# First attention in 32 steps per image, with the scores of a unit beside the weighing of the one before it, across images

## The chip, the core and the metric

The kernel runs on one core of one Trainium2 chip. The metric is the device time of one execution in microseconds, as the median of several runs. The profile is of one further execution, with its own time.

## What is computed

Eight images of 32 x 32 positions and 256 channels pass two layers. The first normalises each image in groups of eight channels and adds, to the input, a 3 x 3 convolution (192 channels) and an attention with eight heads of width 8 (64 channels):

```
logits = einsum('bnid,bnjd->bnij', qf, kf)
logits = logits + rel_w + rel_h          # from rel = einsum('bnxyd,md->bnxym', q, rel_k), in x and in y
weights = softmax(logits, axis=-1)
attn = einsum('bnij,bnjd->bnid', weights, vf)
x = x + concat([conv_out, attn @ attn_w + attn_b])
```

The second layer takes the 1024 positions as tokens: layer norm, one attention head of width 128 with a residual, then a mixture of eight experts of which each image uses two, and a last layer norm. The experts are a separate stage behind all images, and the change leaves it alone.

## The kernel before

Everything up to the experts lies in one hand-ordered program: the order of calls in the source is the order on each engine. Image after image goes through `first_layer` (L676) and `second_layer` (L803).

**The first attention.** Query times key and both relative terms are one matmul. Queries, their products with the relative tables and the maxima stand as rows of a feature tile F (128 rows, two key halves, four heads, 512 queries); keys and one-hot rows stand in KM. An image has four units (two halves of the queries, two groups of four heads). A unit (`Unit`, L493) first loads F from DRAM with six DMAs. `score` (L516) makes the logits of 128 queries of one head in PSUM (two matmuls, L522) and VectorE takes their maximum (L529); a unit has 16 scores. `fold` (L533) splits the maxima, turns them and writes them into F with four DMAs (L548). `weigh` (L553) makes the logits once more, transposed and with the maximum taken off (L558), and ScalarE takes the exponential (L565); a unit has eight steps of four weighings. `gather` (L567) multiplies with the values (four column groups at once, L573), and `settle` (L584) divides.

**The steps.** `first_layer` runs over steps. Step s has two scores of unit s // 8 and four weighings of the step that lies ten steps back (`lead = NT + LAG`). Twelve scores of an image's first unit are already taken beside the second attention of the image before, so its steps run from 6 to 42: four with scores alone, 22 with both, ten with weighings alone, one last. Between them `fill.send(us)` puts in other matmuls: the convolution of this and then of the next image (`convolve_tile`, L477, 36 matmuls of fp32 as the profile counts them, one PSUM bank for all), and chains of small work: `token_mean` of the image before, `normalise` of the next (from step 12, L302), `project` (L610), which makes the inputs of the second attention from half an image.

**The features.** After the weighings, `queries` (L381) copies the queries out of the tile kqh into the tile scr (eight DMAs, L388) and to DRAM (four, L395), and GpSimd makes a second order of them (L400). `keys` (L405) loads the next image's keys into KM with four DMAs of eight rows (L407). `features` (L411) multiplies the queries with the relative tables: per group of heads and per direction 32 small matmuls into a two-bank tile `lg`, two ScalarE copies of the high part (L436), two VectorE subtractions for the low part (L437), and stores to DRAM (L440, L444) from a tile of which there are three. These pieces stand between the matmuls of the second attention, where ScalarE and VectorE have its softmax.

**Queues and buffers.** Nearly all DMAs are issued on SP, in program order: a DMA that waits holds those behind it. PSUM has two double banks `lg`, two banks `st` for weighings, one `mi` for convolution and values, one `po`. SBUF has three tiles of F's size, which go round among units, scr and the projected queries and keys of the second attention:

```
        def f_tile(name, dt=FR):
            return work.tile([P, 2, HG, 512], dt, tag="F", name=name, bufs=3)
```

Of the kernel before, what the change touches and what calls it, by code (L numbers as in the profile page):

```python
# [38 lines left out]
def kernel(  # L39
# [67 lines left out]
    with ExitStack() as ph:  # L107
# [30 lines left out]
        def f_tile(name, dt=FR):  # L138
            return work.tile([P, 2, HG, 512], dt, tag="F", name=name, bufs=3)
# [241 lines left out]
        def queries(b):  # L381
            kqb_ = ready.pop(b)
            scr = f_tile("scr").rearrange("p w h s -> p (w h s)")
            qs = scr[:, 0 : 2 * S].rearrange("p (g s) -> p g s", g=NG)
            qx = scr[:, 2 * S : 4 * S].rearrange("p (g s) -> p g s", g=NG)
            for g in range(NG):
                for i in range(4):
                    nc.sync.dma_start(  # L388
                        out=qs.bitcast(FP)[32 * i : 32 * i + 32, g],
                        in_=kqb_[DK + 32 * g : DK + 32 * g + 32, i // 2, :],  # L390
                    )
            fd = fds[b % 2]
            for g in range(NG):
                for c in range(2):
                    nc.sync.dma_start(  # L395
                        out=fd[g].rearrange("(l c p) s -> c p l s", c=2, p=32)[c, :, 0:2],
                        in_=kqb_[DK + 32 * g : DK + 32 * g + 32],
                    )
            for g in range(NG):
                nc.gpsimd.tensor_copy(  # L400
                    qx[:, g].rearrange("p (x y) -> p y x", y=HH), qs[:, g].rearrange("p (y x) -> p y x", x=WW)
                )
            return qs, qx

        def keys(b):  # L405
            for i in range(4):
                nc.sync.dma_start(  # L407
                    out=KMb[8 * i : 8 * i + 8], in_=kds[b % 2][i % 2].rearrange("(d h) s -> d h s", h=NH)
                )

        def features(b, qs, qx):  # L411


            for g in range(NG):
                for which in range(2):
                    pr = lg_tile("prel").rearrange("p a s -> p (a s)")
                    tab, src = ((bhs, qs), (bws, qx))[which]
                    for i in range(32):
                        nc.tensor.matmul(  # L419
                            pr[:, i * 32 : (i + 1) * 32],  # L420
                            lhsT=tab[:, (WW - 1 - i) * HG : (2 * WW - 1 - i) * HG],
                            rhs=src[:, g, i * 32 : (i + 1) * 32],
                            start=True,
                            stop=True,
                        )
                        if i == 15:
                            yield None
                    t = pt_tile("rel", FR).rearrange("p (l s) -> p l s", l=2)
                    for half in range(2):
                        c = slice(half * 512, (half + 1) * 512)  # L430
                        if which == 0:
                            ps, hi, lo = pr[:, c], t[:, 0, c], t[:, 1, c]
                        else:
                            ps = pr.rearrange("p (x y) -> p y x", y=HH)[:, half * 16 : half * 16 + 16, :]
                            hi, lo = (t[:, l, c].rearrange("p (y x) -> p y x", x=WW) for l in range(2))
                        nc.scalar.copy(hi, ps)  # L436
                        nc.vector.tensor_tensor(lo, ps, hi, ALU.subtract)  # L437
                    tb = t.bitcast(FP)
                    if which == 0:
                        nc.sync.dma_start(out=fys[b % 2][g].rearrange("l p s -> p l s"), in_=tb)  # L440
                    else:
                        dst = fds[b % 2][g][R_M * HG : (R_M + 64) * HG].rearrange("(l p) s -> p l s", p=P)
                        for p in (slice(HG, 64), slice(64, P)):
                            nc.sync.dma_start(out=dst[p], in_=tb[p])  # L444
                    yield None
# [47 lines left out]
        class Unit:  # L493


            def __init__(self, b, n):
                self.half, self.g = divmod(n, NG)
                g, cols = self.g, slice(self.half * 512, self.half * 512 + 512)
                self.F = f_tile("F")
# [101 lines left out]
        class Second:  # L601


            def __init__(self, b):
                big = f_tile("nqk", FP).rearrange("p w h s -> p (w h s)")
                self.nT = big[:, 0 : 2 * S].rearrange("p (k s) -> p k s", k=KC)
                self.qk = big[:, 2 * S : 4 * S].rearrange("p (i s) -> p i s", i=2)
                self.v = work.tile([P, NT, U], FP, tag="v1", name="v1")
# [65 lines left out]
        LAG = 2  # L674

        def first_layer(b, units):  # L676
            at = work.tile([P, NT, DK], FP, tag="at", name="at")
            if b > 0:
                fill.chains.append(token_mean(b - 1))
            sec = None  # L680
            more = b + 1 < B
            lead = NT + LAG
            for s in range(units[0].scored // 2, NU * NT + lead + 1):
                u, j = divmod(s, NT)
                w, k = divmod(s - lead, NT)
                g, l = divmod(s - lead - 1, NT)
                score, weigh = u < NU, 0 <= w < NU
                if s % NT == 0 and 0 < u <= NU:
                    units[u - 1].fold()
                    if u < NU - 1:  # L690
                        units.append(Unit(b, u + 1))
                if s == 12 and more:
                    T[b + 1] = load_image(b + 1)
                    fill.chains.append(normalise(b + 1))
                if s == 3 * NT + 4:
                    sec = Second(b)
                    fill.chains.append(project(b, at, sec, 0, (2, 4, 2)))
                if s == 4 * NT + 3 and more:
                    while b + 1 not in ready:
                        fill.send(0.4)  # L700
                    qs = queries(b + 1)
                us = 0.45
                if done[b] < NT:
                    us = max(us, (NT - done[b]) * 3.2 / max(22 - s, 1))
                if score:
                    units[u].score()
                if weigh:
                    units[w].weigh(k, 0)
                if not score:
                    fill.send(0.2)  # L710
                if score:
                    units[u].score()
                if weigh:
                    units[w].weigh(k, 1)
                if score:
                    fill.send(us)
                if 0 <= g < NU:
                    units[g].gather(l)
                if weigh:
                    units[w].weigh(k, 2)  # L720
                if g > 0 and l == 0:
                    units[g - 1].settle(at)
                fill.send(us if score else 0.4)
                if weigh:
                    units[w].weigh(k, 3)
# [3 lines left out]
            rel = None  # L729
            if more:  # L730
                keys(b + 1)
                rel = features(b + 1, *qs)
            fill.send(1.2)
            if more:
                next(rel)
            units[NU - 1].settle(at)
            fill.send(1.2)
            for c in project(b, at, sec, 1, (1, 6, 1)):
                if c is None:
                    fill.send(1.0)  # L740
            if more:
                next(rel)
            return sec, rel

        class Attention:
# [37 lines left out]
            def drain(self, ahead):  # L783
                while self.scored:
                    self.turn()
                    ahead(2)
                while self.turned:
                    self.turned.pop(0).finish()

# [13 lines left out]
        def second_layer(b, sec, rel):  # L803
            more = b + 1 < B
            st2 = work.tile([P, NT, 6], FP, tag="lst2", name="lst2")
            units = []
            if more:
                fill.dense.insert(min(1, len(fill.dense)), values(b + 1))
            pieces = [2]

            def beside():
                if more and pieces[0] < 8:
                    next(rel)
                    pieces[0] += 1
                    if pieces[0] in (4, 8):
                        units.append(Unit(b + 1, pieces[0] // 4 - 1))
                    fill.send(0.6)
                else:
                    ahead(2)

            def ahead(n):
                for _ in range(n if units else 0):
                    units[0].score()
                fill.send(0.6)

            att.beside = beside
            for ib in range(S // IB):

                def finish(pt, rc, ib=ib):
# [7 lines left out]
                    if ib >= 2:  # L837
                        ahead(2)
                    else:
                        fill.send(0.8)  # L840
# [14 lines left out]
            ahead(2)  # L855
            att.drain(ahead)
            sums[b] = st2
            return units
# [36 lines left out]
        with tc.manual_schedule():  # L895
# [4 lines left out]
            rel = features(0, *queries(0))  # L900
            keys(0)
            fill.dense.insert(min(1, len(fill.dense)), values(0))
            units = []
            for g in range(NG):
                for i in range(4):
                    fill.send(1.5)
                    next(rel)
                units.append(Unit(0, g))
            fill.send(5.0)
            for b in range(B):  # L910
                sec, rel = first_layer(b, units)
                units = second_layer(b, sec, rel)
# [275 lines left out]
```

## Time and profile before

| | us |
|---|---|
| median of 3 runs (2893.95 to 2902.46) | 2897.83 |
| the profiled execution | 2906.21 |
| its span, first to last instruction | 2904.4 |
| first weighing of image 0, of images 2 and 4 | 143.7, 729.5, 1299.5 |
| end of the second attention of image 7 | 2356.3 |
| mean clock granted to TensorE, of full speed | 0.96 |

One core has five engines that run on their own and wait for each other by semaphores: PE (TensorE, with PEld for its weights), DVE (VectorE), ACT (ScalarE), POOL (GpSimd) and SP, which here issues DMAs. The page gives each engine's busy time and the chain of work that ended last. A stretch table gives the busy time of each engine between two moments, with the number of instructions in brackets, the granted clock, the mean busy share of the 16 DMA engines and the GB/s moved. A row of the timeline has start, length, engine, line, operation, what is written from what, how many in a row, and in brackets the idle time of the engine ahead of it with what ended it.

### The profile page before, as it was taken

The numbers are of one execution on the slowest core, as the hardware profiler recorded it, in microseconds if no ns is written. First come the engines' busy times: TensorE is split into PE (matmuls) and PEld (weight loads), VectorE is DVE, ScalarE is ACT, GpSimd is POOL, SyncE is SP. The second block draws the span as 40 slices with busy tenths as digits, with TensorE's granted clock in tenths as the row PEclk, the third lists the DMA queues.
The fourth block names the chain that finished last, engine by engine and source line by source line (L and its number), as shares of the span: only waits on it lengthen the run. The fifth ranks groups of instructions, "written<-read, shape, count | busy, mean of one in ns | idle before, by whom it ended". The sixth has DMA issues, their size and how long they took to land.

```text
span 2904.4 us, 30948 instructions
## 1 busy us (share of the span) xinstructions
PE 2560.5 (88%) x12395; PEld 1685.4 (58%) x12395; DVE 1296.2 (45%) x2327; ACT 965.3 (33%) x1679; POOL 301.0 (10%) x196
## 2 busy tenths in 40 slices
PE   4899879997998799979987998799889769999998
PEld 3865665565656555655475556555654346666665
DVE  4454256426643564366335634662457252333232
ACT  0045214531452145214521552154225422223222
POOL 3011001100110011001100110011000021111110
PEclk7899889999999999999999999999999989999999
DMA  3621233133313321342144114312421031112110
GB/s 99 140 56 38 65 80 74 29 70 94 71 31 80 90 56 31 87 97 42 30 90 99 38 36 95 88 38 41 108 55 30 1 106 58 58 58 73 58 51 22
DMA packets 89761, 186.12 MB, mean 64 GB/s; under 512 B 8161, under 2 KB 36714, under 8 KB 87314
## 3 DMA queue, kind: packets, MB, share of 16 engines
q1 hardware_dynamic: 86962, 182.04, 26.6%
q8 instruction: 98, 1.61, 0.2%
q10 hardware_dynamic: 2656, 2.10, 0.2%
q14 instruction: 45, 0.37, 0.0%
HBM read 112.15 MB, written 62.52 MB: 60 GB/s over the span
## 4 chain that ended last, share of the span: by engine, by line
PE 76%; DVE 15%; ACT 5%; DMA 2%; issue 2%; SPq 1%; POOL 0%; ACTq 0%; DVEq 0%
PE pc L481 11%; PE po L573 9%; PE st L558 9%; PE py L1115 8%; PE phd L1097 8%; DVE mx L529 6%; PE lg L522 6%; PE prel L419 4%; PE po L832 4%; PE lg L754 3%; PE pq L653 2%; ACT PT L565 2%; PE tp L772 2%; PE pmean L874 1%; DMA T<-in_x_dram 1%
## 5 line engine op out<-in xcount | busy, mean ns | idle before, releaser
L565 ACT ACTIVATE PT<-st 128x512 f32<-128x512 f32 x1024 | 598.5, 598 | 492.5 <-PE st L558 452.9
L529 DVE TENSOR_REDUCE mx<-lg 128x1 f32<-128x1024 f32 x512 | 603.7, 1217 | 296.0 <-PE lg L522 295.9
L481 PE MATMUL pc<-convw,gpad 128*128 128x192 f32 x2304 | 506.0, 341 | 55.1 <-DVE T L489 33.6
L558 PE MATMUL st<-F,KM 128*128 128x512 f32 x1024 | 479.7, 474 | 19.6 <-ACT PT L565 11.6
L481 PEld LDWEIGHTS pc<-convw,gpad 128*128 128x128 f32 x2304 | 404.3, 196 | 109.5 <-DVE T L489 42.7
L522 PE MATMUL lg<-KM,F 128*128 128x512 f32 x1024 | 345.5, 424 | 73.9 <-ACT pr L760 32.9
L558 PEld LDWEIGHTS st<-F,KM 128*128 128x128 f32 x1024 | 192.2, 190 | 297.3 <-ACT PT L565 177.4
L573 PE MATMUL po<-PT,vk 128*32 128x512 f32 x2048 | 284.0, 617 | 0.0
L522 PEld LDWEIGHTS lg<-KM,F 128*128 128x128 f32 x1024 | 184.4, 190 | 143.0 <-DVE mx L529 50.3
L1115 PE MATMUL py<-w,hT 128*128 128x256 f32 x1024 | 237.3, 385 | 0.0
L1097 PE MATMUL phd<-n2T,w 128*128 128x512 f32 x512 | 222.9, 593 | 0.0
L1115 PEld LDWEIGHTS py<-w,hT 128*128 128x128 f32 x1024 | 189.9, 190 | 45.6 <-issue 22.4
L1122 DVE TENSOR_TENSOR r<-py,n 128x256 f32<-128x256 f32 x64 | 27.2, 425 | 308.4 <-PE py L1115 308.4
L1097 PEld LDWEIGHTS phd<-n2T,w 128*128 128x128 f32 x512 | 97.0, 191 | 115.5 <-issue 108.4
L352 POOL TENSOR_TENSOR T<-T,l0b 128x2048 f32<-128x2048 f32 x8 | 36.5, 4558 | 1145.2 <-PE tpx L311 1145.2
L591 DVE RECIPROCAL rc<-pa 128x16 f32<-128x16 f32 x32 | 8.3, 258 | 307.1 <-PE pa L588 307.1
L760 ACT ACTIVATE pr<-lg,nm 128x1024 f32<-128x1024 f32 x64 | 71.4, 1115 | 201.8 <-DVE nm L758 201.8
L754 PE MATMUL lg<-nqk 128*128 128x512 f32 x256 | 129.8, 633 | 0.0
L437 DVE TENSOR_TENSOR rel<-prel,rel 128x512 fp32r<-128x512 f32 x64 | 44.3, 692 | 190.6 <-ACT rel L436 190.6
L641 POOL TENSOR_TENSOR T<-T,n 128x256 f32<-128x256 f32 x64 | 48.3, 774 | 755.1 <-DVE n L638 755.1
L832 PE MATMUL po<-pt,v 128*128 128x256 f32 x512 | 121.1, 391 | 0.4 <-DVE pt L775 0.4
L1104 ACT ACTIVATE hT<-phd,b1c 128x512 f32<-128x512 f32 x128 | 86.3, 686 | 97.6 <-PE phd L1097 97.4
(223 smaller groups left out, 2441.4 us busy)
## 6 DMA issues: line engine op xcount, KB each, us to landing
F<-fd SPq DMA_DIRECT2D x64, 768.0 KB
fy<-rel SPq DMA_DIRECT2D x16, 1024.0 KB
F<-fy SPq DMA_DIRECT2D x128, 128.0 KB
w<-in_L_ffn_W_dram SPq DMA_DIRECT2D x32, 512.0 KB
T<-in_x_dram SPq DMA_DIRECT2D x8, 1024.0 KB
scr<-kqh SPq DMA_DIRECT2D x64, 128.0 KB
fd<-kqh SPq DMA_DIRECT2D x32, 256.0 KB
KM<-kd SPq DMA_DIRECT2D x32, 256.0 KB
```

Of the source, the lines that this page charges most:

```text
L419: nc.tensor.matmul(pr[:, i * 32 : (i + 1) * 32], lhsT=tab[:, (WW - 1 - i) * HG : (2 * WW - 1 - i) * HG], rhs=src[:, g, i * 32 : (i + 1) * 32],
L481: nc.tensor.matmul(pc[:, 0:CO], lhsT=gflat[:, dx, kc, t * P + dy * WW : (t + 1) * P + dy * WW], rhs=convw[:, (dy * 3 + dx) * KC + kc, :], ...
L522: nc.tensor.matmul(lg[:, a, :], lhsT=self.F[:, a, hl, i * P : (i + 1) * P], rhs=KM[:, self.g * HG + hl, a * 512 : (a + 1) * 512], start=Tr ...
L529: nc.vector.tensor_reduce(self.mx[:, i, hl : hl + 1], lg.rearrange("p a s -> p (a s)"), AX.X, ALU.max, negate=True)
L558: nc.tensor.matmul(st, lhsT=KM[:, self.g * HG + hl, j * P : (j + 1) * P], rhs=self.F[:, j // 4, hl, :], start=True, stop=True,)
L565: nc.scalar.activation(self.pts[j][:, hl, :], st, AF.Exp)
L573: nc.tensor.matmul(self.po[32 * hl : 32 * hl + 32, :], lhsT=vk[:, j, (self.g * HG + hl) * (DH + 1) : (self.g * HG + hl) * (DH + 1) + 32], ...
L754: nc.tensor.matmul(lg[:, h, :], lhsT=q, rhs=k[:, h * 512 : (h + 1) * 512], start=True, stop=True)
L832: nc.tensor.matmul(po[:, 0:IB], lhsT=sec.v[:, jc, :], rhs=pt[:, jc, :], start=jc == 0, stop=jc == NT - 1)
L1097: nc.tensor.matmul(phd, lhsT=ws[k][0][:, kc, f * P : (f + 1) * P], rhs=n2T[:, kc, q * 512 : (q + 1) * 512], start=kc == 0, stop=kc == KC - 1,)
L1104: nc.scalar.activation(hT[:, k * NF + f, :], phd, AF.Gelu, bias=b1c[:, f, k * B + b : k * B + b + 1])
L1115: nc.tensor.matmul(py, lhsT=hT[:, k * NF + f, j * P : (j + 1) * P], rhs=ws[k][1][:, f, :], start=False, stop=k == TOPK - 1 and f == NF - 1,)
```

## The change

The first attention has now 34 steps. In steps 0 to 31 each has four weighings. The two scores of a step run four scores and one unit ahead: unit 1 in steps 0 to 5, unit 2 in 6 to 13, unit 3 in 14 to 21, none in 22 to 25, and unit 0 of the next image in 26 to 33; four scores of its unit 1 follow in the last part of the second attention. To make this possible, the features of the next image move out of the second attention into the fillings of steps 16 to 23, as eight pieces of 16 matmuls. A piece writes one half of what was a double bank, into the single bank `mi`, and the tile `rel` of high and low parts is now one and takes the place of kqh. `keys` is split by groups of heads: group 0 at step 24, group 1 behind the steps. The next image is loaded and normalised from step 0 on, and the convolution must be finished by step 10. The three tiles of F's size have fixed places, `slot % 3`, in place of going round: the next image's queries take the place of unit 1 at step 16, its unit 0 the place of unit 2 at step 24. Before the first image, all features are made, then twenty scores.

```diff
-        def f_tile(name, dt=FR):
-            return work.tile([P, 2, HG, 512], dt, tag="F", name=name, bufs=3)
+        def f_tile(name, slot, dt=FR):
+            return work.tile([P, 2, HG, 512], dt, tag=f"F{slot % 3}", name=name)
...
+        def place(b, n):
+            return n - b
+
+        def keys(b, g):
+            hs = slice(g * HG, (g + 1) * HG)
             for i in range(4):
                 nc.sync.dma_start(
-                    out=KMb[8 * i : 8 * i + 8], in_=kds[b % 2][i % 2].rearrange("(d h) s -> d h s", h=NH)
+                    out=KMb[8 * i : 8 * i + 8, hs],
+                    in_=kds[b % 2][i % 2].rearrange("(d h) s -> d h s", h=NH)[:, hs],
                 )
...
+        def features(b, qs, qx, n):
+            g, which, half = n // 4, n // 2 % 2, n % 2
+            if half == 0:
+                rels[b] = work.tile([P, 2, S], FR, tag="kqh", name="rel")
+            t = rels[b]
+            pr = mi_tile("prel")
...
+            for i in range(16 * half, 16 * half + 16):
+                nc.tensor.matmul(
...
+                if i % 16 < 15:
+                    yield 0.118
...
+            nc.scalar.copy(hi, ps)
+            nc.vector.tensor_tensor(lo, ps, hi, ALU.subtract)
+            if half == 1:
...
+            done["rel", b] = n + 1
+            yield 0.118
...
-        LAG = 2
+        AHEAD = 4
...
+            for s in range(NU * NT + 2):
+                n = AHEAD + 2 * s
+                u, first = n // 16 + 1, n % 16 == 0
+                if s >= 22:
+                    u, first = NU, s == 22
+                score = u < NU or more and 26 <= s < 34
+                weigh, g = s < NU * NT, s - 1
+                gather = 0 <= g < NU * NT
+                if s == 0:
+                    units.append(Unit(b, 2))
+                    if b > 0:
+                        fill.chains.append(token_mean(b - 1))
+                    if more:
+                        fill.chains.append(fetch(b + 1))
+                        fill.chains.append(normalise(b + 1))
+                if first and s > 0:
                     units[u - 1].fold()
+                if s == 8:
+                    units.append(Unit(b, 3))
+                if s == 16 and more:
                     while b + 1 not in ready:
                         fill.send(0.4)
                     qs = queries(b + 1)
+                    i = min(1, len(fill.dense))
+                    for n in range(8):
+                        fill.dense.insert(i + n, features(b + 1, *qs, n))
+                if s == 24:
+                    while more and done.get(("rel", b + 1), 0) < 8:
+                        fill.send(0.5)
+                    if more:
+                        keys(b + 1, 0)
+                        units.append(Unit(b + 1, 0))
+                    sec = Second(b)
+                    fill.chains.append(project(b, at, sec, 0, (2, 6, 2)))
                 us = 0.45
                 if done[b] < NT:
-                    us = max(us, (NT - done[b]) * 3.2 / max(22 - s, 1))
+                    us = max(us, (NT - done[b]) * 3.3 / max(10 - s, 1))
+                if more and 16 <= s < 24:
+                    us = 1.05
...
             if more:
-                keys(b + 1)
-                rel = features(b + 1, *qs)
...
+                keys(b + 1, 1)
+                units.append(Unit(b + 1, 1))
...
             def beside():
...
+                fill.send(1.2)
+
+            def ahead():
+                if more and units[1].scored < AHEAD:
+                    units[1].score()
+                    units[1].score()
+                fill.send(1.0)
```

## The prediction

> **What bounds the kernel now.** I read the page first: busy shares, then the chain that ended last.
>
> ```profile
> PE 2560.5 (88%) x12395; PEld 1685.4 (58%) x12395; DVE 1296.2 (45%) x2327; ACT 965.3 (33%) x1679; POOL 301.0 (10%) x196
> PE 76%; DVE 15%; ACT 5%; DMA 2%; issue 2%; SPq 1%; POOL 0%; ACTq 0%; DVEq 0%
> ```
>
> TensorE is the bound; no other engine is half busy. So a stage is worth the time in which TensorE does not advance. Ends of matmuls are modelled, so I price by distances between starts in the timeline:
>
> ```profile
> 1052.73 0.39 PE L558 MATMUL st<-F,KM 128*128 128x512 f32 x1
> 1052.96 0.81 PE L481 MATMUL pc<-convw,gpad 128*128 128x192 f32 x4
> 1053.70 1.07 PE L573 MATMUL po<-PT,vk 128*32 128x512 f32 x8
> 1054.70 0.50 PE L558 MATMUL st<-F,KM 128*128 128x512 f32 x1
> ```
>
> A scoring or weighing matmul takes 0.23 us, a convolution matmul 0.16, a gather group (eight rows) 1.2 with its hand-over. Other starts give: feature matmul 0.11, transposes 0.11, lg of the second attention and projections 0.43, po and pa there 0.215. Times the counts of one image (128 st, 128 lg, 288 pc, 32 groups, 128 prel, 56 of 0.43, 96 of 0.215, and 240 small ones of 0.11) this is 230 us. Image after image (weigh starts at 729.5 and 1299.5, two apart) takes 285. So 55 us an image are lost. The stretch table says where (image 3):
>
> ```profile
> core 0: us, PE busy (x) PEld busy (x) DVE busy (x) ACT busy (x) POOL busy (x), PEclk, DMA share, GB/s
> 988.80:1016.80 28.00, 21.02 (x86) 12.75 (x85) 16.60 (x34) 0.94 (x4) 0.00 (x0) 0.88 0.39 104
> 1016.80:1130.10 113.30, 104.34 (x555) 65.68 (x554) 72.88 (x100) 54.89 (x97) 16.32 (x12) 0.97 0.19 36
> 1130.10:1168.80 38.70, 36.53 (x190) 17.80 (x190) 2.28 (x5) 24.89 (x44) 4.02 (x2) 1.00 0.25 56
> 1168.80:1196.60 27.80, 24.81 (x154) 20.05 (x149) 7.61 (x25) 2.75 (x6) 5.37 (x5) 1.00 0.30 38
> 1196.60:1271.00 74.40, 64.45 (x347) 49.68 (x347) 38.47 (x59) 19.53 (x35) 0.00 (x0) 0.98 0.47 113
> ```
>
> Scores alone (ACT 0.94 us busy), scores and weighing, weighing alone (DVE 2.28), the tail, second attention. Length less priced work: 12.5, 15.5, 5.5, 5.3, 14.3 us lost.
>
> **What it gives, per image.** Scores alone: gone but for two steps and four late scores, 12.5 to 1: 11.5. Steps: of 15.5 + 5.5, steps 0 to 17 lose 7.5 (normalisation, convolution tiles), which stays; the projection in steps 18 to 22 loses 9.3 beside a fold, later in steps 24 to 29 perhaps 3.7; weighing alone 0.4 a step, two unfilled steps for nine. So 21 to 12: 9. Second attention: the features leave it, and most scores (two waited 2.3 us each behind ACT pr L760); its own hand-overs, 8, stay: 6.5. Tail: 0. Sum 27; from 20 (the projection still loses its 9) to 34.
>
> **What it costs.** I follow the built order of each engine for a middle image, from 0 = the last weighing of step 15.
>
> *Queries.* They take the place of unit 1's tile, so they cannot start before 0. Before, this lay among weighing-only steps, and the features came 50 us later.
>
> ```profile
> 855.73 6.02 SPq L388 DMA_DIRECT2D scr<-kqh  x8
> 861.79 3.25 SPq L395 DMA_DIRECT2D fd<-kqh  x4
> ```
>
> Group 0 is four of the eight: issued in 3.0, down by about 4.4 (the POOL cast of group 1 at 863.63 was released by the last). TensorE has only 1.7 us before the first feature matmul (two pairs of scores, two weighings, two convolution matmuls): wait 2.7. POOL's casts are needed in step 18: hidden. The first feature piece then ends at 9.2. Its ScalarE copy writes the buffer of kqh, which the fd copies still read, until 13.3:
>
> ```profile
> 862.00:869.00 7.00, 6.31 (x33) 2.85 (x32) 0.91 (x3) 4.81 (x10) 3.23 (x2) 1.00 0.84 179
> 869.00:871.00 2.00, 1.97 (x12) 0.83 (x12) 0.00 (x0) 1.69 (x3) 0.00 (x0) 1.00 0.00 0
> ```
>
> (869.0 - 855.73 = 13.3.) Copy and subtraction follow, and the next piece has the only bank, so it starts at 15.0: wait 5.8. Behind the waiting copy on ScalarE stand the exponentials of step 17, which TensorE could not have fed anyway. Both 8.5; from 7 to 11.
>
> *Eight pieces through one bank.* A piece is 16 matmuls, its copy and subtraction free the bank, and in the built order the next piece's first matmul follows directly. Nearest rows:
>
> ```profile
> 912.01 0.59 ACT L436 CAST rel<-prel 128x512 fp32r<-128x512 f32 x1 [2.08 <-PE prel L419]
> 912.63 0.69 DVE L437 TENSOR_TENSOR rel<-prel,rel 128x512 fp32r<-128x512 f32 x1 [8.09 <-ACT rel L436]
> ```
>
> From the last matmul that is 1.6 us on idle engines; in the steps the copy stands behind up to one exponential (0.6), the subtraction behind a maximum (1.2): 1.6 to 2.9, I take 2.0. Seven boundaries (the last to a convolution tile): 14, from 11 to 20. The single rel tile is a further bound: the next pair's copy waits for the store, 4 to 5 us (fd<-rel issued 924.66, traffic over at 929.6), but a piece itself takes 4.3 to 4.8 with the steps' other matmuls, so this adds nothing.
>
> *The next image's first unit.* Its tile (unit 2's place) is free after step 23, and SP reaches its loads only after the last feature store and four KM copies. From T, the last subtraction: stores issued to T+1.1 and moved by T+5, KM issued to T+2.4, F after that. TensorE does steps 24 and 25 (7.2 us) and wants F at T+7.6. The rows:
>
> ```profile
> 884.00:898.00 14.00, 12.44 (x84) 11.52 (x83) 5.24 (x21) 0.41 (x2) 0.05 (x1) 1.00 0.47 57
> 960.00:971.50 11.50, 8.57 (x47) 6.74 (x48) 6.58 (x9) 2.91 (x6) 0.00 (x0) 1.00 0.92 183
> ```
>
> KM alone keeps half the engines (0.47) busy 17 us, so 8.5 for one group; an F unit takes 12.5 from issue (958.8) to 971.3. By the F row alone, plus the stores ahead, F is there at T+16.5, a wait of 9. The Trainium skill, DMA: Bandwidth & Descriptors (Why a DMA increments its semaphore by 16 and not by 1; Queues, rings and completion order) says that an eight-row copy runs on the eight lowest-numbered engines and that each engine takes its ring in order. Then F's share on those waits for KM: T+5+8.5+10.5 = T+24, a wait of 16.4. The 0.47 agrees with eight engines; no run here has F behind KM. I take 14, nearer the rule; ends 7 and 18.
>
> *Clock.* PEclk is 0.88 in the scores-alone stage and 1.00 where TensorE is full. The skill (TensorE: Matmul & The Clock Gate, Part 1) halves the clock after an idle window of 3.4 us. By the row alone I would book nothing new; by the rule the long waits each cost half a window: 2.5, from 1 to 7.
>
> *Nothing:* T's load comes earlier in the image, with 15 us of TensorE work behind its issue in step 2 against 15.7 between issue and use before (1011.8, 1027.5). Fold to weighing is two steps as before. Uncovered, T would cost a few us.
>
> Sum 2.7 + 5.8 + 14 + 14 + 2.5 = 39 against 27: +12 an image. Seven images have a successor: +84. The prologue changes little (weighing starts 143.7; I see 4 less). The last image has no features: 12.7 less of scores alone, about 5.5 more in twelve steps with no convolution left: -7. In all +73. The profiled execution took 2906.2 (span 2904.4), the median of the runs 2897.8, 8.4 less: 2979, and on the median 2971.
>
> **The rivals.** (1) As summed, 2971, own range 2930 to 3030: 0.55. For it speaks that every wait stands in the built order. (2) Hidden loads: F does not queue behind KM and the clock holds, 14 + 2.5 become 7 + 1: +3.5 an image, 24 - 11 = +13: 2911. 0.18. (3) Queues on ScalarE and VectorE raise the hand-overs to 20, F at 18: +22 an image, 154 - 11 = +143: 3041. 0.08. (4) The other side: the bank hand-over is hidden. At the seven boundaries in steps 16 to 23, if copy and subtraction end while TensorE does a step's other matmuls, they cost 0.2 instead of 2.0: 12.6 less, new waits 26.4 against 27, so -4 and the -11 of both ends remain: 2883; with (2) as well 2823. It decides from about 0.5 us a boundary down (10.4 saved). For it: half the boundaries lie near a weighing; against it: the next piece follows without one in the order. 0.19. That the steps are not equal after all is inside (1): the step list has four weighing-only and two scores-only steps.
>
> **Numbers.** Predicted 2971. About 0.3% is what a measurement here can tell from no change, so faster is below 2889, slower above 2907: faster 0.17, same 0.05, slower 0.78. Range 2880 to 3035: it leaves out about 0.1 on each side.
>
> **What would show it.** prel waiting on DMA scr, about 2.7 us, seven times; ACT rel behind a DMA, and PE prel L430 on DVE rel, 2 us, some fifty times; PE lg waiting on DMA F or KM 9 to 16 us, seven times; PEclk 1.00 where scores stood alone; POOL and ACT totals unchanged. Wrong: no DMA wait before lg, or waits on DVE rel below 0.5 us.

## The result, and the profile after

| | us |
|---|---|
| kernel before, median beside it | 2900.14 (2893.95 to 2905.29) |
| changed kernel, median of 4 runs | 3197.89 (3190.49 to 3204.41) |
| ratio | 1.1027, 95% interval [1.0993, 1.1061] |
| span of the profiled execution, mean clock | 3202.6, 0.883 (before 2904.4, 0.960) |

Slower, as forecast, but by about 298 us where +73 was forecast. It lies above the range's upper end of 3035. First the two lines of the page that the prediction began with:

```profile
PE 2709.0 (85%) x12395; PEld 1825.4 (57%) x12395; DVE 1289.7 (40%) x2327; ACT 966.7 (30%) x1679; POOL 300.2 (9%) x196
...
PE 74%; DVE 13%; DMA 6%; SPq 3%; ACT 2%; issue 1%; POOL 0%; ACTq 0%; DVEq 0%
```

The instructions are the same in number on every engine. DVE, ACT and POOL are busy as long as before (1296.2, 965.3, 301.0); PE is busy 148.5 us longer with the same 12395 matmuls. Work that is the same and takes longer points to the clock, and the mean granted clock is indeed 0.883 where it was 0.960. DMA has risen from 2% to 6% of the chain. The stretch table of image 3 shows where. Its rows are the end of the second attention, steps 0 to 10, 16 to 23, 24 and 25, and 26 to 31.

```profile
core 0: us, PE busy (x) PEld busy (x) DVE busy (x) ACT busy (x) POOL busy (x), PEclk, DMA share, GB/s
1132.10:1137.30 5.20, 4.08 (x21) 3.30 (x20) 3.44 (x6) 0.37 (x1) 0.00 (x0) 1.00 0.26 107
1137.30:1210.20 72.90, 62.04 (x327) 38.52 (x327) 39.69 (x68) 28.34 (x52) 10.64 (x7) 1.00 0.21 51
1230.50:1310.00 79.50, 63.91 (x259) 45.07 (x258) 21.88 (x26) 24.14 (x42) 3.94 (x2) 0.60 0.24 66
1310.00:1336.10 26.10, 11.85 (x53) 6.62 (x52) 4.07 (x17) 5.50 (x11) 0.00 (x0) 0.70 0.80 140
1336.10:1376.50 40.40, 34.86 (x171) 20.48 (x169) 19.18 (x21) 15.83 (x27) 5.39 (x5) 0.92 0.02 5
```

The stretch with scores alone (28.0 us before, at 0.88) has become 5.2 at 1.00: that part came as forecast. In steps 16 to 23, where the features now lie, the clock is 0.60. Its PE is "busy" 80% of the time, but the work in it, priced at full clock, is 38 us. In steps 24 and 25 TensorE stands still for more than half of the time at a DMA share of 0.80.

The list of what engines waited for has a total in us, the number of waits, and the longest (prel is the bank of a feature piece, lg that of a score, pc that of a convolution tile, T the image):

```profile
PE prel L430 <- DVE rel L447: 83.2, 44, 7.3
PE lg L534 <- DMA F<-fy: 78.5, 6, 14.0
PE pc L493 <- DVE T L501: 66.4, 38, 3.4
...
PE prel L430 <- DMA scr<-kqh: 24.2, 8, 5.0
```

That is the whole execution, with all that lies ahead of image 0. The same list for steps 16 to 23 of image 3 alone:

```profile
PE prel L430 <- DVE rel L447: 9.5, 6, 2.0
PE prel L430 <- DMA scr<-kqh: 2.8, 1, 2.8
PE prel L430 <- DVE mh L548: 1.7, 1, 1.7
PE pc L493 <- DVE rel L447: 1.4, 1, 1.4
```

Every wait that the prediction named is there. The copies into scr cost 3.0 us each (forecast 2.7), F 13 us (14; one more wait of 14.0 has no releaser in the trace). A bank hand-over costs 1.4 to 2.8 us in images 1 to 6 (2.0). The longest wait of prel, 7.3 us, lies ahead of image 0's first weighing. In images 1 to 6 TensorE stands still for 16.1 us of steps 16 to 23, where 22.5 were forecast. In the timeline of image 3 these are the rows:

```profile
1230.19 5.03 SPq L389 DMA_DIRECT2D scr<-kqh  x8
...
1234.69 0.59 PE L430 MATMUL prel<-scr,th 128*128 128x32 f32 x4 [2.81 <-DMA scr<-kqh]
...
1242.66 0.58 ACT L446 CAST rel<-prel 128x512 fp32r<-128x512 f32 x1 [0.37 <-DMA fd<-kqh]
1243.28 0.69 DVE L447 TENSOR_TENSOR rel<-prel,rel 128x512 fp32r<-128x512 f32 x1 [0.79 <-ACT rel L446]
```

Copy and subtraction take what they took before (0.59 and 0.69). The first copy is released by the reads of kqh, as the prediction said, but it had waited for them only 0.37 us: the piece before it ended late, and the next piece waited 1.9 us in place of 5.8. So the waits are not what the prediction missed; here they are shorter than it had them.

### The profile page after: what moved, and what is told of

Its sections match the earlier page's. It is cut to its first block, busy times and chain, and to the rows that moved or that the text cites. A ratio compares the mean times of both kernels' runs of the same rounds, so it can differ in the third digit from the quotient of the medians.

```text
span 3202.6 us, 31085 instructions
## 1 busy us (share of the span) xinstructions
PE 2709.0 (85%) x12395; PEld 1825.4 (57%) x12395; DVE 1289.7 (40%) x2327; ACT 966.7 (30%) x1679; POOL 300.2 (9%) x196
## 4 chain that ended last, share of the span: by engine, by line
PE 74%; DVE 13%; DMA 6%; SPq 3%; ACT 2%; issue 1%; POOL 0%; ACTq 0%; DVEq 0%
PE pc L493 11%; PE st L570 9%; PE po L585 9%; PE py L1140 7%; PE phd L1122 7%; PE lg L534 7%; DVE mx L541 5%; PE prel L430 5%; DMA F<-fy 4%; PE po L854 3%; PE lg L781 3%; PE pq L665 2%; PE tp L799 2%; DVE rel L447 1%; PE py L1137 1%
## 5 line engine op out<-in xcount | busy, mean ns | idle before, releaser
L493 PE MATMUL pc<-convw,gpad 128*128 128x192 f32 x2304 | 507.0, 348 | 98.6 <-DVE T L501 66.4
L570 PE MATMUL st<-F,KM 128*128 128x512 f32 x1024 | 526.0, 518 | 10.1 <-ACT PT L577 9.4
L493 PEld LDWEIGHTS pc<-convw,gpad 128*128 128x128 f32 x2304 | 419.5, 203 | 169.2 <-DVE T L501 77.6
L534 PE MATMUL lg<-KM,F 128*128 128x512 f32 x1024 | 370.8, 451 | 120.3 <-DMA F<-fy 78.5
L570 PEld LDWEIGHTS st<-F,KM 128*128 128x128 f32 x1024 | 221.0, 218 | 306.8 <-issue 198.7
L585 PE MATMUL po<-PT,vk 128*32 128x512 f32 x2048 | 321.8, 703 | 0.0
L534 PEld LDWEIGHTS lg<-KM,F 128*128 128x128 f32 x1024 | 212.3, 215 | 176.2 <-issue 94.5
L430 PE MATMUL prel<-scr,th 128*128 128x32 f32 x512 | 108.4, 344 | 64.8 <-DVE rel L447 40.2
L430 PEld LDWEIGHTS prel<-scr,th 128*128 128x128 f32 x512 | 113.9, 308 | 76.0 <-DVE rel L447 42.7
L430 PE MATMUL prel<-scr,tw 128*128 128x32 f32 x512 | 93.5, 312 | 55.0 <-DVE rel L447 43.0
L430 PEld LDWEIGHTS prel<-scr,tw 128*128 128x128 f32 x512 | 100.6, 269 | 64.9 <-DVE rel L447 29.7
```

Of the source, the lines that this page charges most:

```text
L430: nc.tensor.matmul(pr[:, (i % 16) * 32 : (i % 16 + 1) * 32], lhsT=tab[:, (WW - 1 - i) * HG : (2 * WW - 1 - i) * HG], rhs=src[:, g, i * 32 ...
L493: nc.tensor.matmul(pc[:, 0:CO], lhsT=gflat[:, dx, kc, t * P + dy * WW : (t + 1) * P + dy * WW], rhs=convw[:, (dy * 3 + dx) * KC + kc, :], ...
L534: nc.tensor.matmul(lg[:, a, :], lhsT=self.F[:, a, hl, i * P : (i + 1) * P], rhs=KM[:, self.g * HG + hl, a * 512 : (a + 1) * 512], start=Tr ...
L570: nc.tensor.matmul(st, lhsT=KM[:, self.g * HG + hl, j * P : (j + 1) * P], rhs=self.F[:, j // 4, hl, :], start=True, stop=True,)
L585: nc.tensor.matmul(self.po[32 * hl : 32 * hl + 32, :], lhsT=vk[:, j, (self.g * HG + hl) * (DH + 1) : (self.g * HG + hl) * (DH + 1) + 32], ...
```

## The experiments

**Theory W:** the waits add up, and stand in the way of work that the prediction thought hidden. **Theory M:** TensorE's clock stays halved while the small feature matmuls run, so everything between them takes twice as long. To weigh them, each run's trace is summed in one way: the length of a stage, less its matmuls priced at full clock as in the prediction ("lost"), and the time in which the granted clock was half (0.50 of full speed), per image, as the mean of images 1 to 6. Each run stands beside runs of the kernel before on the same chip.

| run | us | ratio, 95% | steps 16-23: length | lost | at half clock | steps 24-25: lost |
|---|---|---|---|---|---|---|
| before | 2900 | | 46.2 | 9.9 | 6.8 | 0.7 |
| after | 3197.89 | 1.1027 [1.0993, 1.1061] | 79.7 | 41.8 | 62.6 | 17.1 |
| no_copy | 3012.6 | 1.0371 [1.0221, 1.0521] | 52.4 | 14.6 | 21.6 | 15.5 |
| wide8 | 3073.31 | 1.0580 [1.0549, 1.0611] | 61.7 | 23.2 | 9.7 | 17.5 |
| wide16 | 3093.72 | 1.0676 [1.0645, 1.0708] | 64.8 | 26.9 | 10.8 | 17.1 |
| one_fill | 3126.7 | 1.0764 [1.0733, 1.0795] | 70.9 | 32.7 | 33.2 | 16.7 |
| rel_pt | 3185.87 | 1.0967 [1.0929, 1.1006] | 80.0 | 42.2 | 63.0 | 17.3 |
| km16 | 3163.27 | 1.0884 [1.0828, 1.0940] | 79.7 | 41.9 | 63.3 | 13.9 |
| late28 | 3112.31 | 1.0708 [1.0665, 1.0752] | 78.6 | 40.8 | 60.2 | 2.4 |
| mix | 2991.73 | 1.0294 [1.0254, 1.0333] | 70.7 | 15.7 | 20.2 | 16.0 |
| mix_late | 2937.29 | 1.0106 [1.0060, 1.0153] | 70.1 | 15.1 | 19.1 | 1.1 |
| mix_rel | 2922.73 | 1.0076 [1.0055, 1.0096] | 69.5 | 14.5 | 17.9 | 0.6 |
| best3 | 2881.1 | 0.9938 [0.9921, 0.9954] | 68.3 | 13.3 | 16.1 | 1.4 |
| best2 | 2910.63 | 1.0032 [1.0014, 1.0050] | 68.1 | 18.9 | 25.8 | 1.4 |
| best_pro | 2882.87 | 0.9946 [0.9929, 0.9962] | 69.0 | 14.0 | 17.5 | 0.8 |

(The runs from mix on have more convolution in steps 16 to 23, so there the lost time is to be compared, not the length.)

**no_copy: the matmuls without the waits behind them.**

```diff
-            nc.scalar.copy(hi, ps)
-            nc.vector.tensor_tensor(lo, ps, hi, ALU.subtract)
-            if half == 1:
+            if b < 2:
+                nc.scalar.copy(hi, ps)
+                nc.vector.tensor_tensor(lo, ps, hi, ALU.subtract)
+            if half == 1 and b < 2:
```

> From the third image on the features are still multiplied, but their ScalarE copies, VectorE subtractions and stores are left out (so those images use the relative terms of earlier ones). In steps 16 to 23 no piece waits for a bank or a buffer any more; the small matmuls, the queries' copies and the load of the next unit stay. Theory W (the waits leave TensorE idle, and that halves its clock): granted clock in steps 16 to 23 back near 1.0, about 10 us of half clock per image in place of 75, time near 2900. Theory M (32-column matmuls count as little activity, whatever the waits): those steps stay at half clock, about 40 us per image, only the waits (about 15 to 20 us an image) go: near 3090.

Measured between the two, at 3012.6. Without hand-overs the half clock does not vanish, it falls from 62.6 to 21.6 us. One row of this kernel, just behind its wait for scr, speaks for M, the next one against it:

```profile
1179.40:1193.10 13.70, 13.54 (x52) 9.10 (x52) 2.45 (x2) 3.46 (x6) 3.91 (x2) 0.50 0.49 107
1193.10:1224.20 31.10, 30.27 (x204) 21.95 (x202) 11.00 (x13) 14.87 (x26) 0.00 (x0) 1.00 0.01 2
```

First TensorE is occupied for 13.54 of 13.70 us, and the clock is still 0.50. Then it is back, and it holds for the rest of these steps, though 106 of the 204 matmuls are feature matmuls and only two are convolution. It is the same in each of images 1 to 6: one stretch at half clock behind the wait for scr, of 10.2 to 47.8 us, and no second one in these steps. So neither theory alone is right: narrow matmuls delay the return of the clock, and the waits between them send it down again.

**wide8: the waits with other matmuls.** Eight matmuls of 512 columns in place of sixteen of 32: about the same time at full clock (8 x 0.23 against 16 x 0.11), same banks, copies, subtractions and stores, other values.

```diff
-            for i in range(16 * half, 16 * half + 16):
+            for i in range(8):
                 nc.tensor.matmul(
-                    pr[:, (i % 16) * 32 : (i % 16 + 1) * 32],
+                    pr,
...
-                    rhs=src[:, g, i * 32 : (i + 1) * 32],
+                    rhs=src[:, g, c],
```

> Each piece of 16 matmuls of 32 columns is replaced by 8 matmuls of 512 columns, which take the same 1.85 us at full clock (so the relative terms are not those of the reference). Waits, copies, stores and their places stay. Theory W: TensorE still idles at each hand-over, the clock stays halved in steps 16 to 23, time within 40 us of 3198. Theory M: with full matmuls the clock stays at 1.0 outside the two longest waits, half clock falls from about 92 to under 40 us per image, time near 3060.

M's number came nearly, and the half clock of a whole image fell from 91.0 to 35.8 us, under M's 40. TensorE has more columns to multiply and the kernel is 125 us faster than the changed one.

**one_fill: a piece in one filling.** All 16 matmuls of a piece stand together in the first filling of a step, the second stays empty.

```diff
                 if more and 16 <= s < 24:
-                    us = 1.05
+                    us, us2 = 1.9, 0.0
```

> In steps 16 to 23 all 16 matmuls of a piece are sent in the step's first filling and none in the second, so the copy and the subtraction end while TensorE does the gather and the later weighings. The bank hand-overs, 12 us an image by the waits on VectorE, should fall under 4. Theory W: with the waits the half clock goes too, about 30 us an image in all: near 2990. Theory M: the clock stays halved, 10 us an image: near 3125.

M's number came, 3126.7, but not on M's grounds: the half clock did not stay, it fell from 62.6 to 33.2 us an image. Nor did the hand-overs fall as expected; the waits of prel on DVE rel rose to 113.6 us in 53 waits. The number of us waited does not by itself rank these kernels.

**rel_pt: no wait for kqh.**

```diff
-                rels[b] = work.tile([P, 2, S], FR, tag="kqh", name="rel")
+                rels[b] = pt_tile("rel", FR).rearrange("p (l s) -> p l s", l=2)
```

> The tile of high and low parts takes its place among the three tiles of the exponentials again, not that of kqh, so the first copy need not wait for the queries' twelve DMAs. By the sum of the prediction this saves 5.8 us an image, 40 us: near 3155; if that long wait is what starts the half clock, several us more per image: near 3100 (theory W); if not, 3155 or, should the exponentials now wait for a tile, 3200 (theory M says nothing of it).

The 7.3 us wait is gone (longest 2.0), and 12 us came of it in the whole kernel where 40 or more were expected. In the profiled executions the gain lies in image 0, counted from the start to the end of its second attention (461.2 us against 478.0); images 1 to 6, from end to end, take 326.5 against 327.1 each. There the wait had already shrunk: the hand-over behind the first piece took 1.4 to 2.8 us before, and takes 1.5 now.

**wide16: columns or instructions?** wide8 changed the number of matmuls and weight loads too. Here both stay, and only the columns rise from 32 to 256 (again other values).

```diff
-                    pr[:, (i % 16) * 32 : (i % 16 + 1) * 32],
+                    pr[:, (i % 2) * 256 : (i % 2 + 1) * 256],
...
-                    rhs=src[:, g, i * 32 : (i + 1) * 32],
+                    rhs=src[:, g, c][:, (i % 2) * 256 : (i % 2 + 1) * 256],
```

> Sixteen matmuls of 256 columns in place of sixteen of 32 (which columns are multiplied is changed; the same banks, copies, waits and stores). By the scoring rows (0.23 us for 512 columns) one takes 0.115 us, beside 0.11 for one of 32, so a piece has the same number of matmuls and weight loads and the same length at full clock. Theory N (few columns: the array hardly works while a new weight block is loaded for each): half-clock time of steps 16 to 23 falls from 62.6 to 10 to 15 us an image as with eight of 512 columns, 3070 to 3090 us. Rival L (the many short matmuls with their weight loads, whatever their columns): it stays above 40 us, 3140 to 3200 us.

The half clock is N's, 10.8 us, and the time, 3093.72, is 4 us above N's range. The kernel waits longer than the changed kernel (prel on DVE rel 104.0 us in 44 waits, lg on DMA F 103.8 in seven) and is 104 us faster. The stretch tables of image 3 say why. First the changed kernel, from the moment its clock fell:

```profile
1236.50:1253.60 17.10, 15.19 (x55) 11.84 (x55) 5.06 (x7) 5.10 (x9) 2.17 (x2) 0.50 0.29 63
1253.60:1257.00 3.40, 1.44 (x14) 1.12 (x16) 1.77 (x2) 1.07 (x2) 0.00 (x0) 1.00 0.14 57
1257.00:1287.70 30.70, 26.50 (x97) 19.08 (x89) 9.20 (x9) 8.90 (x15) 0.00 (x0) 0.50 0.19 62
```

Then wide16, from the same moment:

```profile
1183.80:1187.20 3.40, 3.40 (x14) 1.42 (x15) 0.00 (x0) 0.50 (x1) 1.89 (x1) 0.50 0.91 200
1187.20:1194.00 6.80, 4.21 (x30) 3.57 (x32) 3.05 (x3) 3.07 (x6) 2.09 (x1) 1.00 0.49 107
1194.00:1197.40 3.40, 3.40 (x15) 1.61 (x14) 0.06 (x1) 0.60 (x1) 0.00 (x0) 0.51 0.00 0
```

In both the clock falls after a wait. With 256 columns it is back after 3.40 us, each time (in images 1 to 6 together, 17 times of 18); with 32 it stays down for 17.10, then 30.70 us, although PE counts as busy for 15.19 and 26.50 of these.

**km16: KM in 16 rows.** Is F held up by the eight-row copies ahead of it?

```diff
-            for i in range(4):
+            for i in range(2):
                 nc.sync.dma_start(
-                    out=KMb[8 * i : 8 * i + 8, hs],
-                    in_=kds[b % 2][i % 2].rearrange("(d h) s -> d h s", h=NH)[:, hs],
+                    out=KMb[16 * i : 16 * i + 16, hs],
+                    in_=kds[b % 2].rearrange("l (d h) s -> (l d) h s", h=NH)[:, hs],
```

> The next image's keys go into KM with two DMAs of 16 rows in place of four of 8 rows, same bytes; nothing else changes. Theory Q (F waits because eight engines are held by the eight-row copies): the wait of lg on DMA F, 13 us an image, falls to 6 to 9, about 3160 us. Rival B (F and the feature stores need that time by themselves): the wait stays at 12 to 14, 3190 to 3200 us.

```profile
PE lg L534 <- DMA F<-fy: 65.5, 7, 10.2
```

Q's time came, 3163.27. The F wait fell to 9.4 us on average where it was 13.2 (92.5 in seven, the one without a releaser included), just above Q's 6 to 9, and the loss of steps 24 and 25 by 3.2 us. Fewer issues are not the reason: SP is busy with the copies into KM for 3.79 us in the changed kernel's image 3 and for 3.62 here. Where the other 9 us of F wait lie, in F's own transfer or in the stores ahead of it, no run took apart.

**late28: the next image's scores two steps later,** with more convolution in steps 24 to 27, and four of the scores behind the last `settle`.

```diff
-                score = u < NU or more and 26 <= s < 34
+                score = u < NU or more and 28 <= s < 34
...
+                if more and 24 <= s < 28:
+                    us = 1.35
```

> The next image's first scores begin in step 28 instead of 26, four of them go behind the last settle, and the fillings of steps 24 to 27 become 1.35 instead of 0.45; the features stay as they are. Theory (the F wait is only a matter of distance, and the convolution matmuls put in its place are work that steps 0 to 10 need anyway): the waits on DMA F fall from 78.5 to under 15 us, 10 to 13 us an image with the half clock behind them, 3100 to 3125 us. Rival (the wait moves to the later scores or to the tail's projection): 3170 to 3200 us.

The time is as expected, 3112.31; the waits on DMA F are 17.1 us in all, where under 15 were expected. The convolution done there also relieves steps 0 to 10: waits of pc on DVE T fall from 66.4 to 30.8 us, the loss of those steps from 15.7 to 10.8.

**mix: wide matmuls between the narrow ones.** In steps 16 to 23 the fillings follow a list: the rest of the convolution tile under way, then two pieces, a convolution tile in two halves, two pieces, and so on.

```diff
-                    i = min(1, len(fill.dense))
-                    for n in range(8):
-                        fill.dense.insert(i + n, features(b + 1, *qs, n))
+                    rest = fill.dense.popleft()
+                    fs = [features(b + 1, *qs, n) for n in range(8)]
+                    cs = [fill.dense.popleft() for n in range(3)]
+                    slots = [(rest, 99)]
+                    for n in range(4):
+                        slots += [(fs[2 * n], 99), (fs[2 * n + 1], 99)]
+                        if n < 3:
+                            slots += [(cs[n], 9), (cs[n], 99)]
```

> Steps 16 to 23 have a fixed list of fillings: the rest of the convolution tile under way, then two pieces of features and one convolution tile in two halves, in turn; three tiles more than before lie there, and as many fewer later. A piece always ends at a filling's end, so that weighings or a gather group stand ahead of the next user of the bank. Theory C (half clock needs both: narrow matmuls and the waits between them): half-clock time of steps 16 to 23 falls from 62.6 to under 15 us an image and the waits on DVE rel from 83 to under 30 us, about 2900 us (2860 to 2950). Rival N (32-column matmuls halve the clock wherever sixteen stand together): half-clock time stays above 35 us, 3040 to 3100 us.

Half clock fell to 20.2 us, not under 15, and the time to 2991.73, above C's range and below N's. The waits on DVE rel fell to 19.8 us, 11 waits. Most of the half clock that stays in image 3 lies around a stall in step 17. This is mix_late (same fillings):

```profile
1139.20 0.80 PE L570 MATMUL st<-F,KM 128*128 128x512 f32 x1 [4.34 <-ACT PT L577]
1139.80 3.43 PE L430 MATMUL prel<-scr,th 128*128 128x32 f32 x16
...
1156.04 1.85 PE L430 MATMUL prel<-scr,tw 128*128 128x32 f32 x16
```

The weighing waits for an exponential, which waits on ScalarE behind the first copy, which waits for the reads of kqh. A piece takes 3.43 us at half clock and 1.85 at full.

**mix_late** has the fillings of mix and the later scores of late28.

> The fixed fillings of the kernel mix, and the later first scores of the kernel late28, in one. If both gains are independent, 10 us an image below mix: about 2820 us (2780 to 2870), below the kernel before. Rival (convolution is used up too early: second attention and steps 0 to 10 run without it, and its waits come back there): no better than mix.

2937.29, 54 us off mix. late28 alone took 86 us off the changed kernel, so the two gains add only in part, and the start was higher than expected.

**mix_rel** is mix_late with rel in a tile of the exponentials.

> The kernel mix_late with the high and low parts of the features in one of the three tiles of exponentials in place of kqh's. Theory: what is left of half clock in steps 16 to 23 (19.1 us an image) hangs on one wait, the first copy behind the reads of kqh, with ScalarE's exponentials queued behind it (PE st on ACT PT, 4.3 us in image 3); without it that half-clock time falls under 8 us and an image is 5 to 7 us shorter: 2890 to 2905 us. Rival (the exponentials wait instead for the tile that rel holds): no change, 2930 to 2945 us.

2922.73, 15 us less, but again in image 0 (446.4 against 462.3); images 1 to 6 take 288.5 against 289.0. The stall is gone, and the half clock fell only from 19.1 to 17.9. In image 3 the first two pieces stand behind a wait of 2.01 us for scr and still take 3.11 and 3.43 us, and a later wait of 1.19 us for the subtraction is new. So the theory that all hung on one stall fell.

**best3** adds KM in 16 rows to mix_rel; **best2** has two convolution tiles in place of three there, and the last four pieces one behind the other; **best_pro** spreads the four convolution tiles of the prologue over its eight pieces.

> The kernel mix_rel, and KM in two DMAs of 16 rows. The F wait in step 28 (5.7 us in image 3 of mix_late) falls by the 3 to 4 us that 16 rows gave alone: 3 us an image below mix_rel, 2870 to 2885 us. Rival (F is not what the score waits for there): equal to mix_rel within 5 us.

> The kernel best3 with two convolution tiles in steps 16 to 23 in place of three, and the last four pieces of features one behind the other. For: steps 0 to 10 keep more convolution under the maxima and lose less (14 us an image with three tiles, 11 with none but later scores), 10 to 15 us below best3. Against (the last pieces without wide matmuls between them lose the clock again): 15 to 30 us above best3.

> The kernel best3 with the four convolution tiles of the prologue spread over all eight pieces of image 0 (one ahead of every pair) in place of the first four pieces. If the last pieces there lose the clock like steps 16 to 23 did, 5 to 10 us below best3; if the prologue's loss is in its loads, no change.

best3 takes 2881.1 us, less than both kernels (0.6% below the kernel before), and 42 us below mix_rel where some 20 were expected: with the F wait of step 28 the half clock behind it goes too (steps 26 to 31: 5.1 us against 10.2). Its image 3 between two waits in steps 16 to 23, and in steps 24 and 25:

```profile
1099.60:1120.10 20.50, 18.83 (x126) 14.82 (x125) 7.62 (x11) 6.77 (x13) 0.00 (x0) 1.00 0.17 61
...
1155.50:1165.90 10.40, 10.40 (x58) 7.10 (x59) 3.93 (x17) 5.17 (x11) 0.00 (x0) 0.90 0.99 204
```

Narrow pieces beside convolution keep a clock of 1.00, and with F loading at a DMA share of 0.99 TensorE does not stop. best2 shows the other side: with the last four pieces bare, 25.8 us are at half clock in place of 16.1, and it takes 30 us more. In its image 3 the clock holds through three bare pieces; behind a wait of 1.42 us for the fold it falls, and stays down for 17.1 us, with the fourth. best_pro changes nothing that can be told.

## Why the prediction was right in direction and wrong in size

The lost time of a middle image, by the prediction's terms, and as measured in the changed kernel:

| us per image | forecast | measured |
|---|---|---|
| scores alone and second attention | 10.3 (28.3 in the kernel before, less 11.5 and 6.5) | 4.8 |
| steps 0 to 15 | 7.5 | 16.0 |
| steps 16 to 23, TensorE standing still (scr, kqh, hand-overs) | 22.5 | 16.1 |
| clock: matmuls of these steps, beyond their price at full clock | 2.5 | 25.7 (41.8 less 16.1) |
| F in steps 24 and 25 | 14 | 17.1 |
| steps 26 to 31 (projection) | 4.5 | 10.2 |
| tail | 5.8 | 7.2 |
| sum | 67 | 97 |

Against 55 before that is +42 an image where +12 was forecast; for images 1 to 6 it makes 251 us. Image 0 is 61 us longer (478.0 against 416.9), image 7 14 shorter: 298 in all.

**Right:** the gain of removing scores alone (larger than forecast: 23.5 where 18 were booked), the place of every wait, and the sizes of the waits for scr and the bank. Rival (4), the hidden hand-over, is excluded: in images 1 to 6 each of the 36 waits of prel on DVE rel is 1.4 us or more, where that rival needs 0.5. The direction did not hang on the clock: with 256 columns (wide16) images 1 to 6 still take 312.1 us where the kernel before takes 285.3.

**Right in part by luck:** F. The wait of 13 us for 14 forecast is a difference of two times that were both too early in the sum. In image 3:

```profile
1309.42 1.02 SPq L455 DMA_DIRECT2D fd<-rel  x2
1310.53 3.79 SPq L412 DMA_DIRECT2D KM<-kd  x4
...
1320.92 0.51 PE L570 MATMUL st<-F,KM 128*128 128x512 f32 x1 [0.45 <-ACT PT L577]
1335.10 1.19 PE L534 MATMUL lg<-KM,F 128*128 128x512 f32 x2 [13.67 <-DMA F<-fy]
```

Counted from the last subtraction (the first row starts 0.03 us behind it), TensorE wanted F after 12.0 us (forecast 7.6) and had it after 25.7 (21.6); the copies into KM alone took 3.8 us to issue, where the sum had 1.3. That F queues behind KM on eight engines was a rule weighed against a row; km16 shows that it is a part, 3 to 4 of 14 us. The wait for the reads of kqh was put at 5.8 us and is 1.4 to 2.8 in images 1 to 6: in image 3 the reads ended 12.5 us after the queries' first issue (forecast 13.3), while the first piece ended at 11.9 and not at 9.2.

**Wrong: the clock, the step that failed.** It read: "By the row alone I would book nothing new; by the rule the long waits each cost half a window: 2.5, from 1 to 7." This prices the loss of the clock and takes its return for granted. Measured, the term is 25.7 us an image in steps 16 to 23 alone, since everything in them, weighings and gathers too, ran mostly at half clock. The Trainium skill (TensorE: Matmul & The Clock Gate, Part 1) has the clock back after one busy window of 3.4 us; wide8 and wide16 agree (3.40 us at half, then 1.00). With 32-column matmuls it did not come back for 17.1 and 30.7 us. The prediction's rule for the loss, from the same page, asks for an idle window of 3.4 us; here a wait of 2.81 us was enough. In wide16 the term is 8.2 us (26.9 lost, 18.7 of them standing still), so 17.5 of the 25.7 us hang on the columns; its waits are longer by 2.6. The row in which the prediction saw the pieces was that of the second attention, where they stood between wide matmuls at a clock of 0.98. That the moved matmuls would now be most of TensorE's filling, between waits, was in its own list of steps.

**Too small: steps 0 to 15,** by 8.5 us. They were taken over as they were; with convolution to be done by step 10 in place of 22 and the image's normalisation in the same steps, convolution tiles wait for VectorE: pc on DVE T 66.4 us in 38 waits, where before it was 33.6 in 30. late28 takes some 5 of the 8.5 back by moving convolution elsewhere, so the crowding is a cause; the rest was not separated. **Steps 26 to 31,** by 6: 8.2 us of them are at half clock behind the F wait; no run took this apart from the projection's waits for VectorE. Of image 0's 61 us, rel_pt takes 17 back, so the wait for kqh costs more there, where little else is to be done; best_pro shows no effect of the order of the prologue's tiles in best3.

## What to carry to other kernels

Price the return of the clock as well as its loss: after a wait, ask which matmuls come first, and whether they stream enough columns to bring it back soon. Narrow matmuls that are moved from among wide ones into steps of their own change their price without any change in themselves. Two things helped here: no waits between them (no_copy), or wide matmuls between them, with each group ending where other work covers the hand-over (best3). When the page shows more PE time for the same instructions, compare the granted clock stage by stage before counting waits, since a kernel with more waiting (wide16, 104 us on DVE rel) can be the faster one.

## What was not expected of the hardware

The granted clock does not go by what the profile counts as a busy TensorE. By the distances between starts at full clock, a matmul with 128-row weights and 32 columns takes 0.11 us and one of 256 columns 0.12; yet behind a wait the first kind left the clock at 0.50 through 13.54 busy us of 13.70 (no_copy), and the second had it back after 3.40. At equal number of matmuls, and nearly equal length, columns alone (32 against 256) made 62.6 or 10.8 us of half clock an image, and 104 us of the kernel's time.

Narrow matmuls did not pull a full clock down by themselves. In no_copy it held at 1.00 for 31.10 us with 106 feature matmuls among 204, and no wait for a bank or buffer. What these runs show is a loss behind waits (2.81 us in the changed kernel, 1.42 in best2), and a slow return while the matmuls behind them are narrow. How many columns in how much time bring the clock back was not measured, nor whether a stream of feature matmuls alone, without weighings and gathers between them, would hold it.
